# Down products with the low part last, and a row maximum queued behind a low part, in a fused feed-forward and attention kernel

## The chip, the cores and the metric

The kernel runs on one core of a Trainium2 chip. The metric is device time in microseconds (us), the median of several executions. A core has five engines that work side by side, each through its own queue in order: TensorE (PE in the profile; its weight loads are PEld), VectorE (DVE), ScalarE (ACT), GpSimd (POOL) and SyncE (SP, which here issues DMAs). An instruction waits at the head of its queue for what it needs, and everything behind it waits with it.

## The reference

A feed-forward layer, an attention layer and the same feed-forward layer again, each added to its input, on 4096 tokens of 256 features:

```python
x = x + 0.5 * ffn(layernorm(x))
x = x + attn(layernorm(x))
x = x + 0.5 * ffn(layernorm(x))

def ffn(x):
    # routed: 8 experts, each token to its 2 best, at most 640 tokens an expert
    gate = silu(einsum('ech,ehi->eci', xg, rg))
    up = einsum('ech,ehi->eci', xg, ru)
    eout = einsum('eci,eih->ech', gate * up, rd)
    # shared, for every token, 2048 inner features
    shared = silu(x @ sg) * (x @ su) @ sd
    return shared + routed

def attn(x):
    # groups of 64 tokens, 16 heads of 16 features, causal; q and k are normalised
    att = softmax(where(causal, q @ k.T / 4, -big))
    return (att @ v) @ w_proj
```

Inputs and result are float32.

## The kernel before

**Two-part numbers.** Every operand of a large product is kept as two 16-bit floats, a high part and what the high part leaves, the low part. A product of two such operands is made of three matmuls, in the order of `TERMS` (L35): high by high, high by low, low by high, the first of a pair being the left operand.

**Four phases.** Phase a (to about 268 us): the shared feed-forward part of blocks 0 to 3 of the first layer (a block is 512 tokens), with the normalising and routing of all tokens beside it. Phase b (to 590): the 8 experts of the first layer. Phase c (to 1420): the shared part of the first layer's blocks 4 to 7 and of the second layer's blocks 0 to 6, with the 32 attention tiles (128 tokens each) and the second layer's routing beside it. Phase d: the experts of the second layer and its last shared block.

**A chunk.** The inner features go by chunks of 128: 16 in a shared block, 8 in an expert. `gate_up` (L350) makes six matmuls of the gate into one PSUM bank, six of the up part into the next (`pgu`, a ring of three banks, L50). Of the gate comes `sl`: with `tanh` set, as in phase c, a Tanh on ACT (L367) and an addition and product on DVE (L368); else a Silu on ACT (L371). DVE multiplies by the up part (L373), ACT casts the product to its high part `hh` (L375), and DVE subtracts to make the low part `hl` (L376). `shared` and `experts` put off the chunk's down products by one chunk: `defer` (L97) keeps them and emits those of the chunk before.

**The down products.** `down` (L379) goes through the token tiles of a chunk (4 in a shared block, 5 in an expert) and makes three matmuls for each, with `hh`, `hh` and `hl` on the left, all of them adding to the tile's half of a PSUM bank. A block has two such banks, an expert three. They are read after the last chunk: L417 in a shared block (two instructions on DVE), L507 and L509 in an expert (on ACT and DVE).

**An attention tile.** `attn_tile` (L567) is a generator, written as a row of steps: load and normalise, q, k and v products, q and k to a layout with doubled rows (`QK`, L616 to L624), transposes by DMA, scores and mask (L636, L639), the maximum of each row of scores (`amx`, L644, on DVE over 128 x 1024 values), its subtraction (L645, POOL), the exponential (L653, ACT), the split of it into two parts (L655, L656), a transpose by DMA (`ET`), the products with v (`py`, L667), the normalising (L670, L673), the output product (`pao`), the second layer's normalising and routing products (`pl`). Its steps run in turns with those of a shared block: `drive` (L783) takes one round of tile steps for every three steps of the block, which is one chunk.

**What sets the order.** The program's text is only the order in which instructions are handed over. A scheduler that models each engine's time puts every engine's queue together; it may place any instruction ahead of another that it doesn't depend on, on PE too, so that in the built queue the matmuls of one `down` stand between those of other groups. Two means bind it: what an instruction reads and writes, and `issue_after`, which places an instruction behind a given one in its engine's queue (used by `behind`, L200).

Of the kernel before, what the change touches and what calls it, by code (L numbers as in the profile page):

```python
# [14 lines left out]
AF = mybir.ActivationFunctionType  # L15
ALU = mybir.AluOpType
AX = mybir.AxisListType
# [3 lines left out]
P = 128  # L21
H = 256
# [4 lines left out]
XP = UP * WS  # L27
# [10 lines left out]
class Net:  # L38
    def __init__(self, ctx, tc):
        self.tc = tc  # L40
        self.nc = nc = tc.nc
        pool = lambda name, bufs, **k: ctx.enter_context(tc.tile_pool(name=name, bufs=bufs, **k))
        self.cst = pool("cst", 1)
        self.wsh = pool("wsh", 1)
        self.tok = pool("tok", YB)
        self.xb = pool("xb", NB)
        self.xe = pool("xe", 2)
        self.sm = pool("sm", 2)
        self.dr = pool("dr", 1, space=DRAM)
        self.ps_gu = pool("ps_gu", 3, space=PSUM)  # L50
        self.pend = None
        self.latest = None
        self.anchor = None
        c = self.cst
        self.tri = c.tile([P, P], BF16, name="tri")
        nc.gpsimd.memset(self.tri, 1.0)
        nc.gpsimd.affine_select(
            out=self.tri, in_=self.tri, pattern=[[1, P]], compare_op=ALU.is_gt,
            fill=0.0, base=0, channel_multiplier=-1)
        self.ones = c.tile([P, P], BF16, name="ones")  # L60
        nc.gpsimd.memset(self.ones, 1.0)
        self.iota8 = c.tile([P, E], F32, name="iota8")
        for e in range(E):
            nc.gpsimd.memset(self.iota8[:, e:e + 1], float(e))
        self.mhalf = c.tile([P, 8], F32, name="mhalf")
        nc.gpsimd.memset(self.mhalf, -0.5)
        self.mone = c.tile([P, 4], F32, name="mone")
        nc.gpsimd.memset(self.mone, -1.0)
        self.e1 = c.tile([P, 4], F32, name="e1")
        nc.gpsimd.memset(self.e1, 2.718281828459045)  # L70
        warm = c.tile([P, 8], F32, name="warm")
        nc.scalar.activation(warm, self.mhalf, AF.Silu)
        tk = self.sm.tile([P, 32], I32, name="tk", bufs=1)
        nc.gpsimd.iota(tk, pattern=[[P, 32]], base=0, channel_multiplier=1)
        self.tokid = c.tile([P, 32], F32, name="tokid")
        nc.vector.tensor_copy(self.tokid, tk)
# [273 lines left out]
    def gate_up(self, wc, x, h, tanh=False):  # L350

        nc = self.nc
        n = x.shape[-1]
        ps = []
        for i in range(2):
            p = self.ps_gu.tile([P, n], F32, name="pgu", tag="gu")
            j = 0
            for k in range(2):
                for (w, a) in TERMS:
                    nc.tensor.matmul(  # L360
                        p, lhsT=wc[:, w, i, k, :], rhs=x[:, 2 * a + k, :], start=(j == 0), stop=(j == 5))
                    j += 1
            ps.append(p)
            if i == 0:
                s = self.hp.tile([P, BT], F32, name="sl", bufs=self.nsl)[:, :n]
                if tanh:
                    nc.scalar.activation(s, p, AF.Tanh, scale=0.5 / XP)  # L367
                    nc.vector.scalar_tensor_tensor(  # L368
                        out=s, in0=s, scalar=1.0, in1=p, op0=ALU.add, op1=ALU.mult)
                else:  # L370
                    self.latest[0] = nc.scalar.activation(s, p, AF.Silu, scale=1.0 / XP).ins  # L371
                yield
        self.latest[1] = nc.vector.scalar_tensor_tensor(  # L373
            out=s, in0=ps[1], scalar=1.0 / XP / (2.0 * XP if tanh else 1.0), in1=s, op0=ALU.mult, op1=ALU.mult).ins
        nc.scalar.copy(h[0], s)  # L375
        nc.vector.tensor_tensor(out=h[1], in0=s, in1=h[0], op=ALU.subtract)  # L376
        yield

    def down(self, outs, nt, h, wd, c, nch):  # L379
        nc = self.nc  # L380
        for t in range(nt):
            o = outs[t // 2][:, (t % 2) * H:(t % 2 + 1) * H]
            for j, (a, w) in enumerate(TERMS):
                nc.tensor.matmul(  # L384
                    o, lhsT=h[a][:, t * P:(t + 1) * P], rhs=wd[:, w],
                    start=(c == 0 and j == 0 and t % 2 == 0), stop=(c == nch - 1 and j == 2),
                    skip_group_check=True)

    def hbuf(self):
        hh = self.hp.tile([P, self.ntok], F16, name="hh")  # L390
# [176 lines left out]
    def attn_tile(self, R, j, x2, new_fb):  # L567

        nc = self.nc
        a = self.at  # L570
# [21 lines left out]
        for i in range(2):  # L592
            nc.scalar.activation(qk[:, i, :], pqk[:, i, :], AF.Square, scale=1.0 / XP, accum_out=ss[:, i:i + 1])
        nc.vector.tensor_scalar(
            out=ss, in0=ss, scalar1=XP ** 2 / H, scalar2=1e-6 * XP ** 2, op0=ALU.mult, op1=ALU.add)
# [6 lines left out]
            out=vs[:, 1, :], in0=pv, scalar=1.0 / XP, in1=vs[:, 0, :], op0=ALU.mult, op1=ALU.subtract)  # L602
        yield
        yield
        for i in range(2):
            nc.vector.scalar_tensor_tensor(
                out=qk[:, i, :], in0=pqk[:, i, :], scalar=ss[:, i:i + 1], in1=self.lnw,
                op0=ALU.mult, op1=ALU.mult)
        QS = self.QK[:, 0:16].rearrange("p (j s) (r a c) -> p j s r a c", s=2, r=2, a=4)
        for i in range(2):  # L610
            if i == 0:
                for r in range(2):
                    src = qk[:, 0, :].rearrange("p (j r c) -> p j r c", r=2, c=16)[:, :, r, :]
                    src = src.unsqueeze(2).to_broadcast([P, 8, 2, 16])
                    s = QS[:, :, r, r]
                    nc.scalar.copy(s[:, :, 0:2, :], src)  # L616
                    self.anchor = nc.gpsimd.tensor_tensor(
                        out=s[:, :, 2:4, :], in0=src, in1=s[:, :, 0:2, :], op=ALU.subtract)
            else:
                s = self.QK[:, 16:24].rearrange("p j (r a c) -> p (j r) a c", r=2, a=4)  # L620
# [3 lines left out]
                    out=s[:, :, 1::2, :], in0=src, in1=s[:, :, 0::2, :], op=ALU.subtract)  # L624
        yield
        QT = a.tile([P, 2, 24, 64], F16, name="QT")
        for g in range(2):
            nc.sync.dma_start_transpose(
                out=QT[:, g], in_=self.QK[g * 64:(g + 1) * 64].rearrange("p j c -> p (j c)"))
        yield  # L630
        yield
        S = a.tile([P, 16, 64], F32, name="S")
        for g in range(2):
            p = self.m1([P, 8, 64], F32, "psc")
            for jj in range(8):
                nc.tensor.matmul(  # L636
                    p[:, jj, :], lhsT=QT[:, g, 2 * jj:2 * jj + 2, :].rearrange("p r q -> p (r q)"),
                    rhs=QT[:, g, 16 + jj, :], start=True, stop=True)
            nc.vector.tensor_tensor(  # L639
                out=S[:, g * 8:(g + 1) * 8, :], in0=p,  # L640
                in1=self.mask.unsqueeze(1).to_broadcast([P, 8, 64]), op=ALU.add)
        yield
        mx = self.sm.tile([P, 16], F32, name="amx")
        nc.vector.tensor_reduce(out=mx, in_=S, axis=AX.X, op=ALU.max)  # L644
        self.anchor = nc.gpsimd.tensor_tensor(  # L645
            out=S, in0=S, in1=mx.unsqueeze(2).to_broadcast([P, 16, 64]), op=ALU.subtract)
        for g in range(2):
# [15 lines left out]
        for g in range(2):  # L663
# [7 lines left out]
            for r in range(2):  # L671
                sl = slice(r * 64, (r + 1) * 64)
                nc.vector.tensor_tensor(  # L673
                    out=Y[sl, g], in0=py[sl, :, r * 16:(r + 1) * 16],
                    in1=rc[sl].unsqueeze(2).to_broadcast([64, 8, 16]), op=ALU.mult)
# [253 lines left out]
```

## Time and profile before

| | |
|---|---|
| median of three runs | 1802.04 us (1801.54 to 1802.3) |
| the profiled execution | 1801.58 us |
| its span, first to last instruction | 1799.6 us |
| mean granted clock of TensorE | 0.999 |

The profile is of that one execution. "Busy" is the time in which an engine had an instruction under way; a matmul's end is modelled, since matmuls are pipelined. A line of a group, wait or timeline names the source line, the engine, the operation, and the tiles as out<-in; what stands behind "<-" in brackets is what the engine waited for and how long. The costliest groups show what a chunk costs on the other engines: L376 on DVE 618 ns in the mean over 512, L373 588 over 512, L375 on ACT 534 over 512, L368 682 over 176, and the maximum L644 1212 over 32. The down products are 4992 matmuls of 273 ns modelled length (2048, 1024, 1280 and 640 by operands), each with a weight load of 98 ns.

### The profile page before, as it was taken

Reading aid. Unit: us, or ns where it says so; the run is one execution under the profiler, and the core shown is the slowest. Engines: PE = TensorE matmul, PEld = TensorE weight load, DVE = VectorE, ACT = ScalarE, POOL = GpSimd, SP = SyncE. Lnnn points to the kernel's source line nnn. Section 1 sums busy time; section 2 is a strip of 40 time slices with the busy share of each in tenths; the row PEclk is TensorE's granted clock in tenths of the full one; section 3 lists DMA queues with packets and bytes.
Section 4 is the critical chain, followed back from the end, with each engine's and each line's share of the span. In section 5 each row is a group of like instructions: output and inputs, shape, how many; then the busy total and the mean of one; then the engine's idle time right before and its main releaser. Section 6 shows DMA issues by size and latency. Waiting matters only on the chain.

```text
span 1799.6 us, 37358 instructions
## 1 busy us (share of the span) xinstructions
PE 1773.4 (99%) x13652; PEld 1199.9 (67%) x13652; DVE 1194.3 (66%) x2905; ACT 951.3 (53%) x2053; POOL 753.5 (42%) x1072
## 2 busy tenths in 40 slices
PE   9999999999999999999999999999999999999998
PEld 5666667777777556665666666566656677777765
DVE  7766546666665668877787778777755566666643
ACT  5433335555554456666666666666333455555542
POOL 3677711211112345676767677676430011122210
PEclk9999999999999999999999999999999999999999
DMA  7334134555543356767676675856212154455420
GB/s 226 105 100 116 39 52 112 119 120 118 115 109 68 70 100 102 131 122 137 124 133 139 115 151 109 147 100 125 60 21 55 39 115 110 110 125 119 103 43 13
DMA packets 437545, 185.16 MB, mean 103 GB/s; under 512 B 302193, under 2 KB 434733, under 8 KB 437360
## 3 DMA queue, kind: packets, MB, share of 16 engines
q1 hardware_dynamic: 418880, 160.81, 40.9%
q0 software_dynamic: 17664, 21.17, 7.0%
q8 instruction: 107, 1.75, 0.4%
q10 hardware_dynamic: 816, 0.79, 0.1%
q14 instruction: 78, 0.64, 0.1%
HBM read 78.16 MB, written 42.21 MB: 67 GB/s over the span
## 4 chain that ended last, share of the span: by engine, by line
PE 40%; POOL 9%; DVE 8%; ACT 5%; issue 5%; DMA 2%; SPq 0%; POOLq 0%; DVEq 0%; ACTq 0%
PE pgu L360 25%; PE po L384 13%; POOL xg L341 2%; DVE hl L376 1%; DVE sl L368 1%; POOL S L645 1%; DVE amx L644 1%; ACT V L649 1%; DMA y<-acc 1%; DVE S L639 1%; ACT sl L367 1%; POOL e L656 1%; DVE sl L373 1%; POOL X L339 1%; POOL rstd L150 1%
## 5 line engine op out<-in xcount | busy, mean ns | idle before, releaser
L360 PE MATMUL pgu<-xb,sgu 128*128 128x512 f16 x3072 | 734.4, 379 | 6.4 <-DVE sl L368 5.6
L375 ACT CAST hh<-sl 128x512 f16<-128x512 f32 (+2 forms) x512 | 273.0, 534 | 544.8 <-DVE sl L373 540.0
L360 PE MATMUL pgu<-xe,wc 128*128 128x384 f16 (+1 forms) x3072 | 497.0, 299 | 0.0
L373 DVE SCALAR_TENSOR_TENSOR sl<-pgu,sl 128x512 f32<-128x512 f32 (+2 forms) x512 | 301.1, 588 | 269.4 <-PE pgu L360 236.2
L360 PEld LDWEIGHTS <-sgu 128*128 128x128 f16 x3072 | 292.7, 98 | 277.0 <-issue 9.0
L376 DVE TENSOR_TENSOR hl<-sl,hh 128x512 f16<-128x512 f32 (+2 forms) x512 | 316.4, 618 | 153.0 <-ACT hh L375 151.6
L384 PEld LDWEIGHTS <-hh 128*128 128x128 f16 x3328 | 321.5, 98 | 104.7 <-ACT hh L375 1.4
L360 PEld LDWEIGHTS <-wc 128*128 128x128 f16 x3072 | 300.6, 98 | 91.9
L384 PE MATMUL po<-sdw,hh 128*128 128x256 f16 x2048 | 349.7, 272 | 1.0 <-ACT hh L375 0.6
L384 PE MATMUL po<-sdw,hl 128*128 128x256 f16 x1024 | 249.1, 273 | 9.9 <-DVE hl L376 9.6
L384 PE MATMUL po<-wd,hh 128*128 128x256 f16 x1280 | 221.7, 273 | 0.0
L510 POOL DMA_INDIRECT out_dram<-eo,eidscatter x40 | 64.6, 1616 | 339.6 <-DVE eo L509 305.7
L371 ACT ACTIVATE sl<-pgu 128x384 f32<-128x384 f32 (+1 forms) x336 | 159.1, 474 | 76.5 <-PE pgu L360 49.7
L384 PEld LDWEIGHTS <-hl 128*128 128x128 f16 x1664 | 162.7, 98 | 51.1 <-DVE hl L376 16.4
L510 POOL DMA_INDIRECT acc<-eo,eidscatter x40 | 64.9, 1622 | 290.6 <-DVE eo L509 257.2
L368 DVE SCALAR_TENSOR_TENSOR sl<-sl,pgu 128x512 f32<-128x512 f32 x176 | 120.1, 682 | 57.0 <-ACT sl L367 55.9
L341 POOL DMA_INDIRECT xg<-X,di x128 | 133.5, 1043 | 45.6 <-issue 22.7
L384 PE MATMUL po<-wd,hl 128*128 128x256 f16 x640 | 147.9, 273 | 0.0
L367 ACT ACTIVATE sl<-pgu 128x512 f32<-128x512 f32 x176 | 104.4, 593 | 31.9 <-PE pgu L360 30.4
L105 ACT ACTIVATE wc<-re 128x512 f16<-128x512 f32 x124 | 78.1, 630 | 60.6 <-PE pgu L360 59.9
L106 DVE SCALAR_TENSOR_TENSOR wc<-re,wc 128x512 f16<-128x512 f32 x124 | 85.6, 690 | 13.9 <-ACT wc L105 13.9
L645 POOL TENSOR_TENSOR S<-S,amx 128x1024 f32<-128x1024 f32 x32 | 63.7, 1991 | 70.3 <-DVE amx L644 69.9
(159 smaller groups left out, 1729.1 us busy)
## 6 DMA issues: line engine op xcount, KB each, us to landing
re<-in_L_ffn_rg_dram SPq DMA_DIRECT2D x124, 128.0 KB, 2.3
re<-in_L_ffn_ru_dram SPq DMA_DIRECT2D x124, 128.0 KB, 2.5
re<-in_L_ffn_rd_dram SPq DMA_DIRECT2D x124, 128.0 KB, 2.5
y<-acc SPq DMA_DIRECT2D x64, 128.0 KB, 2.4
y<-in_L_attn_x_dram SPq DMA_DIRECT2D x32, 128.0 KB, 2.1
acc<-xr SPq DMA_DIRECT2D x16, 256.0 KB, 2.3
out_dram<-xr SPq DMA_DIRECT2D x16, 256.0 KB, 3.1
x<-y SPq DMA_DIRECT2D x28, 128.0 KB, 2.0
```

The lines of the kernel that those rows point to most:

```text
L106: nc.vector.scalar_tensor_tensor(out=lo, in0=src, scalar=WS, in1=hi, op0=ALU.mult, op1=ALU.subtract)
L341: i = nc.gpsimd.indirect_dma_start(out=R["xg"][:, :], out_offset=bass.IndirectOffsetOnAxis(ap=di[:, t, k:k + 1], axis=0), in_=X, in_offset ...
L360: nc.tensor.matmul(p, lhsT=wc[:, w, i, k, :], rhs=x[:, 2 * a + k, :], start=(j == 0), stop=(j == 5))
L367: nc.scalar.activation(s, p, AF.Tanh, scale=0.5 / XP)
L368: nc.vector.scalar_tensor_tensor(out=s, in0=s, scalar=1.0, in1=p, op0=ALU.add, op1=ALU.mult)
L371: self.latest[0] = nc.scalar.activation(s, p, AF.Silu, scale=1.0 / XP).ins
L373: self.latest[1] = nc.vector.scalar_tensor_tensor(out=s, in0=ps[1], scalar=1.0 / XP / (2.0 * XP if tanh else 1.0), in1=s, op0=ALU.mult, op ...
L375: nc.scalar.copy(h[0], s)
L376: nc.vector.tensor_tensor(out=h[1], in0=s, in1=h[0], op=ALU.subtract)
L384: nc.tensor.matmul(o, lhsT=h[a][:, t * P:(t + 1) * P], rhs=wd[:, w], start=(c == 0 and j == 0 and t % 2 == 0), stop=(c == nch - 1 and j == 2),
L510: i = nc.gpsimd.indirect_dma_start(out=R["acc"][:, :], out_offset=bass.IndirectOffsetOnAxis(ap=ids[:, t:t + 1], axis=0), in_=eo, in_offset ...
L645: self.anchor = nc.gpsimd.tensor_tensor(out=S, in0=S, in1=mx.unsqueeze(2).to_broadcast([P, 16, 64]), op=ALU.subtract)
```

## The change

`down` takes the three terms as its outer loop and the token tiles as the inner one: first high by high for every tile, then high by low, then low by high. In the first chunk of a block or an expert (`c == 0`) it does so for two tiles at a time, that is for one PSUM bank. The list `lows` collects the instructions that make low parts, and the maximum over a tile's scores is placed behind the last but one of them in DVE's queue. The list `looks` is filled but not read.

```diff
+        self.lows, self.looks = [], []
...
-                    nc.scalar.activation(s, p, AF.Tanh, scale=0.5 / XP)
+                    self.looks.append(nc.scalar.activation(s, p, AF.Tanh, scale=0.5 / XP).ins)
...
-        nc.vector.tensor_tensor(out=h[1], in0=s, in1=h[0], op=ALU.subtract)
+        self.lows.append(nc.vector.tensor_tensor(out=h[1], in0=s, in1=h[0], op=ALU.subtract).ins)
...
     def down(self, outs, nt, h, wd, c, nch):
-        nc = self.nc
-        for t in range(nt):
-            o = outs[t // 2][:, (t % 2) * H:(t % 2 + 1) * H]
+        nc = self.nc
+        step = 2 if c == 0 else nt
+        for t0 in range(0, nt, step):
             for j, (a, w) in enumerate(TERMS):
-                nc.tensor.matmul(
-                    o, lhsT=h[a][:, t * P:(t + 1) * P], rhs=wd[:, w],
-                    start=(c == 0 and j == 0 and t % 2 == 0), stop=(c == nch - 1 and j == 2),
-                    skip_group_check=True)
+                for t in range(t0, min(t0 + step, nt)):
+                    nc.tensor.matmul(
+                        outs[t // 2][:, (t % 2) * H:(t % 2 + 1) * H], lhsT=h[a][:, t * P:(t + 1) * P], rhs=wd[:, w],
+                        start=(c == 0 and j == 0 and t % 2 == 0), stop=(c == nch - 1 and j == 2),
+                        skip_group_check=True)
...
         mx = self.sm.tile([P, 16], F32, name="amx")
-        nc.vector.tensor_reduce(out=mx, in_=S, axis=AX.X, op=ALU.max)
+        with self.tc.issue_after(self.lows[-2]):
+            nc.vector.tensor_reduce(out=mx, in_=S, axis=AX.X, op=ALU.max)
```

## The prediction, made before the changed kernel ran

> **What bounds the kernel now.** I read the page's first part, then the stages, then the timeline of the one stage that is not full. The page says that PE is the bound, and which waits break it:
>
> ```profile
> PE 1773.4 (99%) x13652; PEld 1199.9 (67%) x13652; DVE 1194.3 (66%) x2905; ACT 951.3 (53%) x2053; POOL 753.5 (42%) x1072
> ...
> L384 PE MATMUL po<-sdw,hl 128*128 128x256 f16 x1024 | 249.1, 273 | 9.9 <-DVE hl L376 9.6
> ```
>
> The windows by stage (columns: start and end, length, busy time of PE, PEld, DVE, ACT, POOL, then clock and DMA) put the holes into one stage:
>
> ```profile
> 18.00:268.00 250.00, 250.00 (x1679) 152.72 (x1677) 156.08 (x489) 101.59 (x210) 147.11 (x308) 1.00 0.36 92
> 268.00:590.00 322.00, 321.61 (x2538) 248.09 (x2536) 202.94 (x451) 174.32 (x408) 63.34 (x39) 1.00 0.48 107
> 590.00:1420.00 830.00, 812.73 (x6462) 508.27 (x6461) 604.93 (x1452) 478.65 (x990) 469.93 (x648) 1.00 0.55 105
> 1420.00:1732.00 312.00, 312.00 (x2486) 242.94 (x2484) 194.20 (x431) 168.33 (x394) 56.94 (x35) 1.00 0.47 106
> ```
>
> The shared blocks of phase a and both runs of experts lose nothing; phase c, where the attention tiles run beside the shared blocks, loses 17.3 us. A matmul's modelled end hides part of a hole, so I went through PE's timeline of phase c by starts: 256 columns take 109 ns to the next start, 512 take 216 (the medians over 4991 and 3072 of them), and what is longer is a hole. From 818 us on, phase c repeats itself every 81.5 us (one shared block of 16 chunks beside four attention tiles), with four holes each time. **Hole A**, once a block, in the timeline at 838:
>
> ```profile
> 836.88 0.68 DVE L639 TENSOR_TENSOR S<-psc,mask 128x512 f32<-128x512 f32 x1
> 837.00 0.62 ACT L375 CAST hh<-sl 128x512 f16<-128x512 f32 x1 [1.95 <-DVE sl L373]
> 837.60 1.22 DVE L644 TENSOR_REDUCE amx<-S 128x16 f32<-128x1024 f32 x1
> 838.36 0.38 PE L384 MATMUL po<-sdw,hh 128*128 128x256 f16 x2
> 838.73 0.68 DVE L376 TENSOR_TENSOR hl<-sl,hh 128x512 f16<-128x512 f32 x1
> 838.90 2.28 POOL L645 TENSOR_TENSOR S<-S,amx 128x1024 f32<-128x1024 f32 x1 [2.47 <-DVE amx L644]
> 839.47 0.28 PE L384 MATMUL po<-sdw,hl 128*128 128x256 f16 x1 [0.73 <-DVE hl L376]
> ```
>
> hh was ready at 837.62, but VectorE did the maximum (1.22) first, so the low part came late: two hh products from 838.36 should end at 838.58, and the first hl product starts at 839.47, 0.89 later. **Hole B**, at 878:
>
> ```profile
> 877.72 0.97 POOL L341 DMA_INDIRECT xg<-X,di  x1 [0.30 <-issue]
> 878.17 1.10 DVE L376 TENSOR_TENSOR hl<-sl,hh 128x512 f16<-128x512 f32 x1
> 878.55 0.38 PE L384 MATMUL po<-sdw,hh 128*128 128x256 f16 x2
> 879.34 0.28 PE L384 MATMUL po<-sdw,hl 128*128 128x256 f16 x1 [0.40 <-DVE hl L376]
> ```
>
> Here the maximum already stands behind hl; hl itself is long. **Holes C and D**, at the change of block:
>
> ```profile
> 895.38 1.46 PE L360 MATMUL pgu<-xb,sgu 128*128 128x512 f16 x6
> 895.73 0.71 ACT L616 CAST QK<-qk 128x256 f16<-128x256 f32 x2 [0.65 <-DVE qk L606]
> 896.34 0.59 ACT L367 ACTIVATE sl<-pgu 128x512 f32<-128x512 f32 x1
> 896.97 0.69 DVE L368 SCALAR_TENSOR_TENSOR sl<-sl,pgu 128x512 f32<-128x512 f32 x1 [0.55 <-ACT sl L367]
> 897.71 1.46 PE L360 MATMUL pgu<-xb,sgu 128*128 128x512 f16 x6 [0.87 <-DVE sl L368]
> 899.56 0.68 DVE L417 SCALAR_TENSOR_TENSOR xr<-po,xr 128x512 f32<-128x512 f32 x1
> 900.16 0.68 DVE L376 TENSOR_TENSOR hl<-sl,hh 128x512 f16<-128x512 f32 x1
> 900.90 0.28 PE L384 MATMUL po<-sdw,hl 128*128 128x256 f16 x1 [0.71 <-DVE hl L376]
> ```
>
> C: the up products of chunk 1 need the bank of chunk 0's gate, whose Tanh waited on ACT behind attention casts: 895.38 + 6 x 0.216 = 896.68 against 897.71, 1.03. D: chunk 0's hl stands behind L417 twice and L639; two hh products from 899.81, and 0.87 lost.
>
> **The change, part by part.** It adds no instruction and no byte: all engine queues of the two builds hold the same instructions. They stand in another order, which the scheduler made, so I laid the built queues side by side.
>
> (1) *Low products last.* In chunks 1 to 15 all 8 hh products now stand ahead of the 4 hl ones, where in most chunks 2 to 4 did. At A and B 8 stand there instead of 2: 6 x 0.109 = 0.65 more cover. At D (chunk 0, two tiles at a time) 4 instead of 2: 0.22. Elsewhere in phase c I added, chunk by chunk, the shift of the first hh and first hl product (in PE work since the chunk's up products) to the distance that the trace shows between the ready operand and its use. In the repeating blocks none outside the holes falls below 0.7; two chunks near 650 us come out under zero, by less than 0.1, as new waits. The number of weight loads stays (one of 98 ns for each of 4992 down products, under 109 ns).
>
> (2) *The maximum behind hl.* In VectorE's queue this moves the maximum past an hl in 7 of 32 tiles, the sites A; in the others it already stands behind the hl that the change names. There hl comes 1.21 us earlier (the mean of L644), behind it nothing shifts, since the same two instructions end at the same time. The maximum comes 0.68 later; who waits for it is POOL's L645, then ACT's exponential, the casts, the transposes of ET and, on PE, the py products. Cover: in the tightest tile of the trace those start 1.9 us after ET landed; without it the 7 tiles would cost up to 7 x 0.68 = 4.8.
>
> Terms, against the profiled execution (1801.58; span 1799.6 and 1.98 around it):
> - A, seven sites (at 757, 838, 920, 1002, 1083, 1165, 1246: 0.35, 0.89, 0.90, 0.90, 0.90, 0.89, 0.19) = 5.0. 1.21 and 0.65 exceed each: all gone, -5.0 (bounds -5.0 and 0).
> - First 130 us of phase c: at 641 0.58 (hh) and 0.55, at 672 0.66, at 686 0.27, at 713 0.36 = 2.4. First products move back 0.62 and 1.27 (at 641), then hl by 0.76, 0.65, 0.38: -2.4 (0 if the new order of the first two attention tiles, whose qk products move up by 8 to 9 us, opens a hole as large).
> - B, six sites (0.19, 0.57, 0.16, 0.17, 0.16, 0.18) = 1.4, covered by 0.65: -1.4.
> - D: 6 x 0.22 = -1.3 of 5.2.
> - C: the edit doesn't touch it, but the order on ACT does: the squares of q and k (0.36 to 0.37 each, with accumulator reads) now stand ahead of both z (0.60), and the last cast (L622, 0.61) ahead of the Tanh. By hand at 891: squares from 891.6 to 892.4 and not 894.2; L594 at 893.1 behind nm; POOL's power 893.3 to 893.9; L606 to 894.9; casts to 895.8; Tanh at 895.8, not 896.34; L368 0.57 earlier. Bounds: 0.61 worse, if only the cast counts, to 1.03 better; I take -0.57 x 6 = -3.4, the value followed through rows.
> - Given back: POOL is busy without a pause that PE could shorten from 865.65 to 892.64 (the e of one tile, scatters, L645, the next e, rstd), and C waits for that rstd. What B saves PE inside this stretch makes PE wait longer at C: +1.4. A lies ahead of it, and at 864.15 POOL idles 3.66 us for the cast of yp, which hangs on PE's py products: A is kept.
> - Tail: PE ends 0.28 earlier, the first L417 starts 0.08 earlier: -0.1.
>
> Sum: -5.0 - 2.4 - 1.4 - 1.3 - 3.4 + 1.4 - 0.1 = -12.2, so 1789.4 for the profiled execution; the median of the runs lies 0.46 above that execution, so 1789.8: I say **1790**. Phase a and the experts have no hole to lose, and the distances counted there stay above 0.4 us: 0.
>
> The Trainium skill (SBUF — State Buffer, Who interferes with whom) says that a VectorE instruction with two SBUF inputs and a GpSimd instruction that reads SBUF shut each other out, the first holding the port to its end, and that a tensor_reduce never contends. The trace agrees: in hole B hl has 1.10 against 0.69 (median of hl rows with POOL idle), and the longest of all is 2.20. By that rule the swap puts the instruction that can be blocked where the one stood that can't.
>
> **The rivals.**
> *hl blocked in its new place*: if at A a POOL instruction stood beside the new hl, it could take 2.20, 1.5 longer; 1.21 + 0.65 - 1.5 leaves 0.36 of each 0.9 won, 2.5 for A instead of 5.0: 1792.3, and with a POOL instruction such as e (2.13) in every case 1794.8. Against: the row at 838.90 shows POOL idle for 2.47 us there.
> *POOL sets the pace*: if the attention chain and not PE decides, A and B are paid back at C, and C's reordering wins nothing: left are 2.4 + 1.3 + 0.1 = 3.8, so 1797.8. For it: the stretch of 27 us above. Against: the 3.66 us of POOL idle ahead of it.
> *It doesn't do what it says*: what PE waits for is not hl but something that comes as late, and the holes keep their size: 1802. Against: hl ends 0.06 ahead of the first hl product in each case.
> *Slower*: the 12 products of a chunk now stand as one block, and 62 groups of six gate or up products in phase c are cut by a whole block, 21 before. A cut gate's Tanh comes up to 1.31 later while the group that reuses its bank comes no later: in each block four groups have their distance from the group three earlier cut, from 5.5 to 7.8 us to 5.1 to 7.1. C's bank was released 5.19 us after its group. If release behind those cuts gets longer than 5.1 to 5.8, each waits like C: 4 x 6 x 1.03 = 24.7, less 12.2: 1814. Against: C's release is the slowest, and the other banks are not behind the attention casts.
>
> **How the numbers follow.** Forecast (1785 to 1794) 0.66; POOL's pace 0.12; hl blocked 0.05; no effect 0.06; slower 0.11. Less than 0.2%, 3.6 us, can't be told from no change. Forecast, hl blocked and two thirds of POOL's pace are faster: 0.79; the rest of it with no effect: 0.10 same; 0.11 slower. The range: below, C gone whole (2.8 more) and nothing given back (1.4): 1785. Above, C worse (3.4 + 3.7 less): 1797, POOL's pace 1798.2 on the runs' scale: 1799.
>
> **What would show it.** Right: PE's wait on hl (9.6) falls below 5, and what is left stands at the change of block; the maximum stands behind hl in every tile; the blocks of phase c come every 79.8 us instead of 81.5. C shows at the second group of a block: 0.5 to 1.0. Wrong: new waits of PE on L368 or L373 at cut groups, or C longer than 1.03 by what A and B gave.

## The result, and the profile after

The changed kernel takes 1792.85 us (median of 5 runs, 1792.66 to 1793.34); the kernel before, on the same chip, 1801.97 (1801.54 to 1802.3). The ratio is 0.9951, 95% interval 0.994 to 0.9962. The forecast was 1790, in a range of 1785 to 1799. The profiled execution took 1792.66, its span 1791.0, with a granted clock of 0.999 as before.

The first lines are from the page of the changed kernel: engines, then the down products of the low part (busy and mean ns of one; idle time of PE just before them, and what ended it).

```profile
PE 1772.8 (99%) x13652; PEld 1201.0 (67%) x13652; DVE 1190.0 (66%) x2905; ACT 944.3 (53%) x2053; POOL 747.1 (42%) x1072
...
L387 PE MATMUL po<-sdw,hl 128*128 128x256 f16 x1024 | 157.0, 273 | 3.9 <-DVE hl L377 3.8
```

Every engine has as many instructions as before, and the wait on the low part has gone from 9.6 to 3.8. That the group is busy for 157.0 instead of 249.1 is no saving: four hl products now stand side by side, and their modelled lengths overlap.

The windows by stage, with the borders moved by the 9 us that phase c became shorter:

```profile
18.00:268.00 250.00, 250.00 (x1676) 152.54 (x1675) 157.37 (x491) 100.71 (x211) 149.04 (x309) 1.00 0.36 93
268.00:590.00 322.00, 321.18 (x2536) 247.91 (x2534) 202.19 (x450) 170.83 (x409) 64.33 (x39) 1.00 0.47 107
590.00:1411.00 821.00, 811.75 (x6467) 508.99 (x6465) 601.46 (x1452) 480.03 (x990) 461.99 (x648) 1.00 0.57 106
1411.00:1723.00 312.00, 312.00 (x2483) 242.80 (x2482) 193.55 (x431) 164.88 (x394) 56.22 (x35) 1.00 0.47 106
```

PE is idle in phase c for 9.25 us (821.00 less 811.75), where it was 17.3. The other stages are as full as they were (321.18 of 322 for the experts, 321.61 before).

As in the prediction, I took each distance between the starts of two neighbouring matmuls, less what the first takes (109 ns for 256 columns, 216 for 512), and call what exceeds 0.1 us a hole. From 18 us to the end:

| holes, us | before | changed |
|---|---|---|
| start of phase c, 575 to 790 us | 6.12 | 7.84 |
| repeating blocks, 790 to 1260 us | 17.52 | 6.99 |
| elsewhere | 0.64 | 0.68 |
| sum | 24.28 | 15.51 |

The sum falls by 8.8 and the span by 8.6, so the holes account for the time. The blocks won more than forecast, the start of phase c got worse.

**Hole A is gone.** Timeline of the changed kernel at 838, the place shown of before:

```profile
837.67 0.68 DVE L377 TENSOR_TENSOR hl<-sl,hh 128x512 f16<-128x512 f32 x1
...
838.27 1.21 DVE L648 TENSOR_REDUCE amx<-S 128x16 f32<-128x1024 f32 x1
...
839.75 0.93 PE L387 MATMUL po<-sdw,hh 128*128 128x256 f16 x7
```

The maximum (L648) stands behind hl (L377). hl is done at 838.35, 1.4 us before even the first hh product; before, PE waited 0.73 for it with only two products ahead of it.

**Holes C and D**, at the change of block:

```profile
893.60 0.70 POOL L599 TENSOR_TENSOR ss<-ss,mhalf 128x2 f32<-128x2 f32 x1 [0.50 <-DVE ss L597]
...
894.33 0.88 DVE L609 SCALAR_TENSOR_TENSOR qk<-pqk,ss,lnw 128x256 f32<-128x256 f32 x2 [0.81 <-POOL ss L599]
...
895.35 0.39 PE L639 MATMUL psc<-QT 128*128 128x64 f16 x8 [0.42 <-DVE qk L609]
...
895.99 0.59 ACT L368 ACTIVATE sl<-pgu 128x512 f32<-128x512 f32 x1
...
896.61 0.69 DVE L369 SCALAR_TENSOR_TENSOR sl<-sl,pgu 128x512 f32<-128x512 f32 x1 [0.47 <-ACT sl L368]
```

C (the up products of chunk 1 behind L369) is 0.25 in each block, not 1.03. Ahead of it stands a new hole of 0.18 to 0.59: the second group of score products needs the PSUM bank that L609 reads, and that hangs on POOL's L599, as C did before. D, one block earlier:

```profile
819.27 0.68 DVE L420 SCALAR_TENSOR_TENSOR xr<-po,xr 128x512 f32<-128x512 f32 x1
...
819.51 0.60 PE L387 MATMUL po<-sdw,hh 128*128 128x256 f16 x4
819.86 0.68 DVE L377 TENSOR_TENSOR hl<-sl,hh 128x512 f16<-128x512 f32 x1
...
820.60 0.39 PE L387 MATMUL po<-sdw,hl 128*128 128x256 f16 x2 [0.49 <-DVE hl L377]
```

hl still stands behind the second read of the old block (L420). Four hh products stand ahead of it instead of two, and the hole is 0.65 instead of 0.87.

**The start of phase c** has holes at two places where before had smaller ones. The first:

```profile
633.16 0.40 ACT L172 CAST xa<-z 128x256 f16<-128x256 f32 x1 [3.68 <-DMA xt<-xa]
633.47 2.50 ACT L653 COPY V<-vs 64x512 f16<-64x512 f16 x4
...
635.99 0.71 ACT L619 CAST QK<-qk 128x256 f16<-128x256 f32 x2
...
636.61 0.61 ACT L625 CAST QK<-qk 128x512 f16<-128x512 f32 x1
637.13 0.61 ACT L376 CAST hh<-sl 128x512 f16<-128x512 f32 x1
...
637.72 1.16 POOL L626 TENSOR_TENSOR QK<-qk,QK 128x512 f16<-128x512 f32 x1
637.77 1.66 DVE L377 TENSOR_TENSOR hl<-sl,hh 128x512 f16<-128x512 f32 x1 [6.08 <-ACT hh L376]
...
637.79 1.05 PE L387 MATMUL po<-sdw,hh 128*128 128x256 f16 x8 [1.62 <-ACT hh L376]
...
639.49 0.61 PE L387 MATMUL po<-sdw,hl 128*128 128x256 f16 x4 [0.64 <-DVE hl L377]
```

Read it from the end: PE waits for hh, then for hl. hh stands on ACT behind the copies of V and the casts of q and k, and all of these behind a cast into `xa`, which has one buffer and waits until the DMA transpose of the tile before has read it. ACT did nothing for 3.68 us, and PE lost 1.78 ahead of hh. The 0.81 behind it is hl's own: hl takes 1.66 beside POOL's L626, where the median of hl with POOL idle is 0.69. At 0.69 it would have ended at 638.46, ahead of the eighth hh product's end (637.79 + 8 x 0.109 = 638.66), and by these rows no hole would be there. L626 is POOL's part of the cast of k; it falls beside hl because the casts of q and k stand just ahead of hh. The second place:

```profile
672.95 2.13 POOL L660 TENSOR_TENSOR e<-S,e 128x1024 f16<-128x1024 f32 x1 [4.63 <-ACT e L659]
...
673.73 1.89 DVE L377 TENSOR_TENSOR hl<-sl,hh 128x512 f16<-128x512 f32 x1 [2.10 <-ACT hh L376]
...
675.55 0.63 DVE L597 TENSOR_SCALAR ss<-ss 128x2 f32<-128x2 f32 x1
676.09 0.41 DVE L604 SCALAR_TENSOR_TENSOR vs<-pv,vs 128x256 f16<-128x256 f32 x1
...
676.55 0.39 PE L639 MATMUL psc<-QT 128*128 128x64 f16 x8 [1.53 <-DVE vs L604]
```

hl takes 1.89 beside POOL's e, and L604, which frees a bank for score products, is queued behind it. PE loses 1.69. Before lost 1.20 at this place in two parts (0.66 for hl, 0.54 for L604). The score products stand ahead of the hl products in PE's queue, so moving the low part back took the first wait away, and PE came to the second one earlier.

### The profile page after: what moved, and what is told of

Read it like the earlier page. It is cut to its first block, busy times and chain, and to the rows that moved or that the text cites. A ratio compares the mean times of both kernels' runs of the same rounds, so it can differ in the third digit from the quotient of the medians.

```text
span 1791.0 us, 37351 instructions
## 1 busy us (share of the span) xinstructions
PE 1772.8 (99%) x13652; PEld 1201.0 (67%) x13652; DVE 1190.0 (66%) x2905; ACT 944.3 (53%) x2053; POOL 747.1 (42%) x1072
## 4 chain that ended last, share of the span: by engine, by line
PE 88%; DVE 3%; POOL 3%; ACT 2%; issue 2%; DMA 1%; SPq 0%; DVEq 0%; POOLq 0%; ACTq 0%
PE pgu L361 55%; PE po L387 28%; PE pqk L702 2%; PE pao L702 1%; PE py L671 1%; PE pv L702 1%; DVE hl L377 1%; DVE sl L369 1%; DMA QT<-QK 1%; PE psc L639 1%; DVE xr L420 1%; DVE sl L374 0%; POOL xg L342 0%; ACT hh L376 0%; ACT sl L368 0%
## 5 line engine op out<-in xcount | busy, mean ns | idle before, releaser
L361 PE MATMUL pgu<-xb,sgu 128*128 128x512 f16 x3072 | 719.6, 379 | 2.2 <-DVE sl L369 1.2
L377 DVE TENSOR_TENSOR hl<-sl,hh 128x512 f16<-128x512 f32 (+2 forms) x512 | 313.9, 613 | 154.2 <-ACT hh L376 151.1
L387 PE MATMUL po<-sdw,hh 128*128 128x256 f16 x2048 | 270.4, 272 | 1.8 <-ACT hh L376 1.8
L387 PE MATMUL po<-wd,hh 128*128 128x256 f16 x1280 | 190.3, 273 | 0.0
L369 DVE SCALAR_TENSOR_TENSOR sl<-sl,pgu 128x512 f32<-128x512 f32 x176 | 120.0, 682 | 67.2 <-ACT sl L368 66.9
L387 PE MATMUL po<-sdw,hl 128*128 128x256 f16 x1024 | 157.0, 273 | 3.9 <-DVE hl L377 3.8
L387 PE MATMUL po<-wd,hl 128*128 128x256 f16 x640 | 115.2, 273 | 0.0
```

Of the source, the lines that this page charges most:

```text
L361: nc.tensor.matmul(p, lhsT=wc[:, w, i, k, :], rhs=x[:, 2 * a + k, :], start=(j == 0), stop=(j == 5))
L369: nc.vector.scalar_tensor_tensor(out=s, in0=s, scalar=1.0, in1=p, op0=ALU.add, op1=ALU.mult)
L377: self.lows.append(nc.vector.tensor_tensor(out=h[1], in0=s, in1=h[0], op=ALU.subtract).ins)
L387: nc.tensor.matmul(outs[t // 2][:, (t % 2) * H:(t % 2 + 1) * H], lhsT=h[a][:, t * P:(t + 1) * P], rhs=wd[:, w], start=(c == 0 and j == 0 a ...
```

## The experiments

Each kernel is compared with runs of the kernel before on its own chip, which took 1801.49 us for experiments 1 and 2, 1804.90 for 3 and 4, and 1801.29 for 5. All edits are against the changed kernel, if not said otherwise. Holes are counted as in the table above.

**1. The parts alone.** Down products with the low part last, without the bound maximum:

```diff
-        with self.tc.issue_after(self.lows[-2]):
-            nc.vector.tensor_reduce(out=mx, in_=S, axis=AX.X, op=ALU.max)
+        nc.vector.tensor_reduce(out=mx, in_=S, axis=AX.X, op=ALU.max)
```

> The low products last, the maximum not bound. In the built queue of VectorE the maximum stands behind the low part at the sites A all the same: with the low products later the scheduler puts it there by itself. On ACT the Tanh of hole C stands ahead of the three casts of QK, the squares of q and k behind z, X and xa. Theory of the holes (PE is the bound, the time is its work and its holes): A and B gone, D 0.65, C 0.25 or less, start of phase c unknown: 1790 to 1793. Theory that the bound maximum brings its own 5 us: 1797 to 1798.

Measured 1798.79 us, ratio 0.9985 (0.9976 to 0.9994). That is outside both ranges and nearer to the rival's; the trace says otherwise. From 901 us to 1225 us it has the holes of the changed kernel, place by place, to within 0.11: with low last, the scheduler by itself puts the maximum behind hl there. Of the 6.0 us of holes that it has more, 4.9 lie at the start of phase c (12.72 against 7.84) and the rest at the first change of block (814 and 824) and at 1246. The first tiles stand in an order that neither kernel has, and there a cast into `xa` that waits for its DMA stands ahead of a Tanh that PE needs. Its timeline on ACT:

```profile
660.98 0.40 ACT L172 CAST xa<-z 128x256 f16<-128x256 f32 x1 [3.77 <-DMA xt<-xa]
661.29 0.59 ACT L368 ACTIVATE sl<-pgu 128x512 f32<-128x512 f32 x1
```

PE lost 1.95 there. Other holes of that start have other causes: 1.62 at 652 stands behind a Tanh that follows a table load (1.28) and an exponential (1.06) on ACT, 1.84 at 682 behind L604, which is queued behind an hl of 1.89. What the bound maximum is worth stayed open until experiment 5.

The bound maximum alone, with the old order of down products:

```diff
     def down(self, outs, nt, h, wd, c, nch):
...
-        step = 2 if c == 0 else nt
-        for t0 in range(0, nt, step):
+        for t in range(nt):
+            o = outs[t // 2][:, (t % 2) * H:(t % 2 + 1) * H]
             for j, (a, w) in enumerate(TERMS):
-                for t in range(t0, min(t0 + step, nt)):
...
```

> The maximum bound behind the low part, the down products in the old order. Holes: A gone (7 sites, 5.0), D 0.87, C 1.03 (ACT's order there is that of before), B as before: 1797, between 1795.5 and 1798. Theory that the attention chain through POOL sets the pace: 1801 to 1802, since nothing of that chain comes earlier and the maximum comes 0.68 later in 7 tiles.

Measured 1796.96, ratio 0.9972 (0.9961 to 0.9984), as expected. Its timeline at the place of hole A:

```profile
838.09 0.69 DVE L377 TENSOR_TENSOR hl<-sl,hh 128x512 f16<-128x512 f32 x1
...
838.70 1.21 DVE L646 TENSOR_REDUCE amx<-S 128x16 f32<-128x1024 f32 x1
...
838.82 0.38 PE L385 MATMUL po<-sdw,hh 128*128 128x256 f16 x2
...
839.04 0.27 PE L385 MATMUL po<-sdw,hl 128*128 128x256 f16 x1
```

The hl product starts 0.22 after two hh products: no hole. All seven sites of A are closed, B stays (0.14 to 0.58), C (1.03) and D (0.87) are as before. The blocks lose 12.77 instead of 17.52. Nothing of A was paid back at C, where the rival by which POOL sets the pace said 1801 to 1802: for hole A that rival is refuted.

**2. Hole D.** Low last over the whole first chunk:

```diff
-        step = 2 if c == 0 else nt
+        step = nt
```

> The changed kernel, with the first chunk of a block term by term over all four tiles too, not two at a time. At D eight high products stand ahead of the first low one, not four. Holes: the high products of tiles 2 and 3 wait some 0.2 for their bank, which the second L417 frees at about the time when the low part begins, then cover the low part; hole D falls from 0.65 to 0.2 to 0.4, 6 sites: 1.5 to 2.7 less than the changed kernel, 1790.1 to 1791.3. Rival, that the bank and not the low part ends hole D: no gain, 1792.8 or more.

Measured 1790.61, ratio 0.9939 (0.9925 to 0.9952): as expected. D goes from 0.65 to 0.27, because the next products are then those of the second bank, which wait for L420: it ends at 820.16, and the first of these products starts at 820.21.

The second read behind the first low part:

```diff
+                    with self.tc.issue_after(self.lows[-1]) if i else nullcontext():
-                    nc.vector.scalar_tensor_tensor(
+                        nc.vector.scalar_tensor_tensor(
...
```

> The changed kernel, with the second L417 of a block bound behind the low part of the next block's first chunk: at D VectorE's queue reads L417, L639, hl, L417. Simple theory (hole D is the low part's lateness alone): hl 0.6 earlier, 6 sites, 3.6 less than the changed kernel: 1789.2. Theory of two holes: the second bank comes free 0.6 later, and the high products of tile 2, behind the low ones of tiles 0 and 1, wait 0.4 for it: 0.43 left of 0.65, 1.3 less: 1791.5.

Measured 1791.31, ratio 0.9945 (0.9931 to 0.9958), as the theory of two holes has it. Its timeline, with the read now in L421:

```profile
819.14 0.68 DVE L377 TENSOR_TENSOR hl<-sl,hh 128x512 f16<-128x512 f32 x1
...
819.39 0.60 PE L387 MATMUL po<-sdw,hh 128*128 128x256 f16 x4
819.74 0.68 DVE L421 SCALAR_TENSOR_TENSOR xr<-po,xr 128x512 f32<-128x512 f32 x1
...
820.48 0.60 PE L387 MATMUL po<-sdw,hh 128*128 128x256 f16 x4 [0.20 <-DVE xr L421]
```

The wait on hl is gone, and the wait on the bank took its place, 0.37 of 0.65. DVE has two results to deliver there, and PE waits for whichever comes second.

**3. The start of phase c.** A second buffer for `xa`:

```diff
-        xa = a.tile([P, 2 * H], F16, name="xa")
+        xa = a.tile([P, 2 * H], F16, name="xa", bufs=2)
```

> The changed kernel with a second buffer for xa (the attention input that is transposed by a DMA), so that ACT's cast xa of tile 1 need not wait until the transpose of tile 0 has landed. Nothing else is edited; near 634 us that cast now stands right behind the one before, and hh and the 12 products behind it stand in the same order. Theory 'a cast that waits for a DMA stands ahead of hh on ACT': the hole of 1.78 ahead of the hh products at 636 falls under 0.4 and the hl wait of 0.81 behind it under 0.4; 2.0 to 2.6 less, 1790.3 to 1790.9. Rival 'the first attention tiles set the pace': the hole moves on to the next group that needs them, the holes from 583 to 760 us still sum to 7.2 or more, and the time is 1792.2 to 1793.4.

Measured 1793.39, where the kernel before took 1804.90 (1804.08 to 1806.61): ratio 0.9937 (0.9923 to 0.995), which is 1790.6 where before takes 1801.97. The interval alone does not part it from the changed kernel's 0.9951. The holes do: 7.84 fall to 4.40 at the start. Timeline at the same place:

```profile
635.75 0.41 ACT L172 CAST xa<-z 128x256 f16<-128x256 f32 x1 [2.24 <-DMA xt<-xa]
...
636.07 0.61 ACT L376 CAST hh<-sl 128x512 f16<-128x512 f32 x1
...
636.71 0.74 DVE L377 TENSOR_TENSOR hl<-sl,hh 128x512 f16<-128x512 f32 x1 [4.35 <-ACT hh L376]
636.73 1.05 PE L387 MATMUL po<-sdw,hh 128*128 128x256 f16 x8 [0.45 <-ACT hh L376]
...
637.62 0.60 PE L387 MATMUL po<-sdw,hl 128*128 128x256 f16 x4
```

With two buffers it is a later tile's cast that waits, for 2.24, and hh stands right behind it. The hole ahead of hh is 0.62 (under 0.4 was expected), that ahead of hl is gone, as hl takes 0.74 and not 1.66, and one of 0.50 follows at L369.

The same buffer in the kernel before:

> The kernel before with the same second buffer for xa. Its first tiles have no cast that waits for a DMA ahead of an hh that PE needs, so by the first theory the buffer is worth nothing by itself: 1801.0 to 1802.4. If the buffer helped in any order (a wait that both kernels have), it would take 2 us here too: 1799.5 or less.

Measured 1803.31, ratio 0.999 (0.9981 to 0.9999), by the medians 1.6 less. So the expectation was wrong: the start's holes fall from 6.12 to 4.01. The timeline of before at 640, read again, shows why:

```profile
640.58 0.40 ACT L171 CAST xa<-z 128x256 f16<-128x256 f32 x1 [4.00 <-DMA xt<-xa]
640.89 0.61 ACT L375 CAST hh<-sl 128x512 f16<-128x512 f32 x1
...
641.53 0.74 DVE L376 TENSOR_TENSOR hl<-sl,hh 128x512 f16<-128x512 f32 x1 [2.66 <-ACT hh L375]
...
641.56 0.39 PE L384 MATMUL po<-sdw,hh 128*128 128x256 f16 x2 [0.42 <-ACT hh L375]
```

The holes of 2.59 after the change (1.78 and 0.81) were 1.13 before (0.58 and 0.55), behind the same wait of `xa`. The change didn't make that wait; the new order put seven ACT instructions (4 copies of V, 3 casts of q and k) between the waiting cast and hh, and POOL's part of the last cast beside hl.

**4. Two more tries at the start, on the same chip.** Low last over the whole first chunk, with the first casts of q in tiles 0 to 3 bound behind the newest hh cast:

```diff
-        nc.scalar.copy(h[0], s)
+        self.highs.append(nc.scalar.copy(h[0], s).ins)
...
-                    nc.scalar.copy(s[:, :, 0:2, :], src)
+                    with self.tc.issue_after(self.highs[-1]) if j < 4 else nullcontext():
+                        nc.scalar.copy(s[:, :, 0:2, :], src)
```

> The version with the low part last in the first chunk too (1790.61, the base of comparison) with the first casts of q in tiles 0 to 3 bound behind the newest hh cast on ACT, xa left with one buffer. Near 634 us hh then stands behind the waiting xa cast and one cast of k, but ahead of the copies of V (2.49) and the casts of q (0.71): about 3 us earlier. Theory 'casts ahead of hh on ACT': the two holes of 1.79 and 0.81 go, 1788.0 (1787.5 to 1788.8). Rival 'the first attention tiles set the pace': the casts come later, so the transposes and the psc products do, and PE waits there instead: 1790.2 to 1792.

Measured 1793.12, ratio 0.9937 (0.9923 to 0.995). By the ratio nothing was won over its base (0.9939), as the rival has it. By the holes the start went from 8.42 to 5.22, as the first theory has it: the 1.79 ahead of hh became 0.58 and the 0.81 ahead of hl 0.14. Between the two readings stand 3.85 us of holes at 1271 to 1334, which all four profiles taken on this chip have in some size (2.68 to 3.85), the one of before with a second `xa` too, and no other profile of this study. By its time this run is inconclusive.

The first shared block of phase c with its down products in the old order:

```diff
-        step = 2 if c == 0 else nt
+        step = 1 if old else 2 if c == 0 else nt
...
-                self.down(outs, 4, h, self.sdw[:, :, c], c, 16)
+                self.down(outs, 4, h, self.sdw[:, :, c], c, 16, tanh and b == NA and src is dst)
```

> The changed kernel, with the down products of the first shared block of phase c (the only one beside the first four attention tiles) in the old order, tile by tile. If the order of the products is what makes the start worse (by the holes 583 to 760 us: 5.8 us before, 7.8 after), the start goes back to about 5 to 6 us and the time to 1790.0 to 1791.3. If the scheduler's order there is chance, and the bound maximum alone is enough to stir it, the start holds 7 to 10 us in some third order: 1792 to 1795.

Measured 1795.28, ratio 0.9947 (0.9933 to 0.996), with 5.45 of holes at the start. The holes agree with the first theory. The ratio, 1792.4 where before takes 1801.97, doesn't, and the 3.69 us at the end of phase c on this chip blur it. It is one more sample of an order and no proof.

**5. Together.** The changed kernel again, and three that use the second `xa`.

> The changed kernel once more, so that the others of this call have it on the same chip: 0.994 to 0.9962 of the kernel before, as in its first runs. No theory is tried by it.

Measured 1792.10 (1791.94 to 1793.47), ratio 0.995 (0.9936 to 0.9963), with 7.87 of holes at the start: the order there is fixed in the built kernel, and its cost repeats to 0.03 us.

Second `xa` and low last over the whole first chunk:

```diff
-        step = 2 if c == 0 else nt
+        step = nt
...
-        xa = a.tile([P, 2 * H], F16, name="xa")
+        xa = a.tile([P, 2 * H], F16, name="xa", bufs=2)
```

> The low part last over the whole first chunk too, and a second buffer for xa. Two theories of two separate waits: 0.35 to 0.4 less in each of six blocks (2.2 as run alone) and 3.4 less holes at the start of phase c (as run alone). If both add up, 5.6 less than the changed kernel (4.5 to 6.2), about 1787.2 where that takes 1792.8. If the second xa only moves the start's waits on (rival: its ratio of 0.9937 was within the interval of the changed kernel's), 2.2 less.

Measured 1787.58 (1786.43 to 1788.57), ratio 0.9921 (0.9907 to 0.9934). That is 4.5 us less than the changed kernel on the same chip, and the two intervals don't touch. The two parts add up, at the low end of what was expected: 2.5 at the start (holes 5.37; alone it was 3.4) and 2.0 in the blocks (5.02). The page has nothing left of the wait that the change was about:

```profile
L387 PE MATMUL po<-sdw,hl 128*128 128x256 f16 x1024 | 155.4, 273 | 0.1
```

Low last and second `xa`, maximum not bound: the diffs of experiments 1 and 3 together.

> Low part last without the bound maximum (1798.79 alone, where the changed kernel had 1792.85), with the second buffer for xa. In the repeating blocks its order is that of the changed kernel; all of the 6 us lay at the start of phase c. Theory 'the bound maximum is worth nothing by itself, and the loss came from casts behind the xa cast that waits for its buffer': the start's holes fall from 12 to about 4 to 5 us, and the time to that of the changed kernel with a second xa: 3 less to 1 more than the changed kernel. Rival 'the bound maximum does protect hl at the start': 3 us or more above the changed kernel.

Measured 1789.10 (1788.53 to 1789.44), ratio 0.9931 (0.9917 to 0.9944), 3.0 less than the changed kernel and 9.7 less than the same kernel with one `xa` (0.9985 there). The start's holes fall from 12.72 to 3.15. So what low last alone lost does not come from the missing bound on the maximum. Not all of it was the wait for that buffer: of the 9.6 us of holes that went, 4.55 stood behind casts into `xa` or in their wake (1.79, 0.81 and 1.95), and the 1.62 and 1.84 named in experiment 1, which have other causes, went with the order too. With two buffers the bound maximum is worth nothing that the times can tell: 0.9931 without it, 0.9937 with it (experiment 3, on the chip that loses time near the end of phase c). By the holes it is worth 0.6 in the blocks (7.9 without, 7.3 with) and nothing at the start (3.15 without, 4.40 with). In five tiles the maximum stands ahead of an hl here, with one hole of 0.38 and one of 0.18 to show for it.

The version with the first chunk and second `xa`, and QK in two copies as well:

```diff
-        self.QK = a.tile([P, 24, P], F16, name="QK")
-        nc.gpsimd.memset(self.QK, 0.0)
+        self.QKs = []
+        for i in range(2):
+            q = a.tile([P, 24, P], F16, name=f"QK{i}")
+            nc.gpsimd.memset(q, 0.0)
+            self.QKs.append(q)
...
+        QK = self.QKs[j % 2]
```

> As the version with the first chunk and the second xa, with QK (the layout that the second DMA transpose reads) in two copies too, so that neither cast of a tile waits for a transpose of the tile before. Theory 'after xa, the next wait at the start is QK's': 0.5 to 1.5 less again at the start (holes of 0.62 and 0.50 at 636 and 638, 0.80 at 673). Rival 'what is left there is the psc groups behind VectorE and the hh casts': within 0.5 of the version with xa alone, or above it where the new order opens others.

Measured 1787.72 (1787.44 to 1788.4), ratio 0.9925 (0.9911 to 0.9938): the rival, within 0.2 of the same version with one QK. The trace has something of both: the hole ahead of hh at 636 fell from 1.24 to 0.42, one of 1.04 ahead of hl opened at 600, and the start sums to 4.9 instead of 5.4. The hole of 0.79 that it keeps at 672 is the one behind hl and L604.

## Why the prediction came out as it did

The direction and the range were right, and the likeliest value was 2.9 us too low. Term by term, in holes, beside what was forecast:

| term | forecast | measured |
|---|---|---|
| A, seven sites | -5.0 | -5.0 |
| B, six sites | -1.4 | -1.4 |
| D, six sites | -1.3 | -1.3 (0.87 to 0.65) |
| C and what is given back | -3.4 + 1.4 = -2.0 | -3.1 (1.03 to 0.25 in six blocks, and 1.6 in new holes at L639) |
| first 130 us of phase c | -2.4 | +2.1 (5.77 to 7.84, from 575 to 790 us, without A's site at 757) |
| tail | -0.1 | -0.3 |
| first chunks of the experts | 0 | +0.3 (0.16 at 271 and at 1414) |
| sum | -12.2 | -8.7 |

Added up before rounding, the holes fall by 8.8.

**The term that was mis-sized is the first 130 us of phase c.** The working took the holes at 641, 672, 686 and 713, saw that the products move back in PE's queue by more than each, and wrote -2.4. It measured the distance from a ready operand to its use and left the ready time where it was. Its upper bound of 0 ("if the new order of the first two attention tiles ... opens a hole as large") was too near as well. The runs showed that at 641 the ready time was set on ACT, by a cast that waits for a DMA, and moving the products couldn't help against what the new order puts behind that cast: 1.78 ahead of hh, and 0.81 ahead of an hl that POOL lengthened. The idle time of ACT, 4.00 us ended by a DMA, was in the trace of before. For the repeating blocks I had followed ACT's order by hand, and there the forecast held but for the size of C; for the first tiles I had looked at PE's order alone. The hole at 672 was taken for one of hl alone; the wait for L604 behind the same hl was not in the sum.

**C was mis-sized the other way.** C itself fell by 0.78 a block and not by 0.57, and fell below the 0.5 to 1.0 named as its sign. What is given back showed, but ahead of C: the 0.18 to 0.59 at L639 hang on POOL's L599, whose place behind e and the two rstd the prediction had named. Each block comes 79.5 us after the one before (the up products behind C start at 897.35, 976.88, 1056.42: 79.5), where 79.8 was said.

**The signs named beforehand.** PE's wait on hl fell to 3.8, below 5, and 2.9 of it stands at the change of block (six times 0.49), right. No maximum is followed directly by an hl on DVE (seven were), right. No new wait of PE at cut gate or up groups in the blocks, so the rival that ended slower has no support in this trace; the bank releases behind such groups were not measured one by one.

**The other rivals.** POOL's pace fell with experiment 1, second kernel. "hl blocked in its new place" did not happen at A, where hl takes 0.68. At the start it did, in the rows of 1.66 and 1.89 above. The 1.66 is new (before, hl took 0.74 there), and it is PE's loss of 0.81. The 1.89 stood at the same place before. The trace agrees there with the Trainium skill (SBUF — State Buffer, Who interferes with whom), by which a VectorE instruction with two SBUF inputs and a GpSimd instruction that reads SBUF contend: hl, with two SBUF inputs, ends at 675.62, about half a microsecond after POOL's e at 675.08. What the 1.89 cost was decided by what stood behind hl in DVE's queue.

**The sum of the parts.** Alone, low last wins 2.7 us and the bound maximum 4.5 by the medians (1801.49 less 1796.96; 5.0 by its ratio); both win 9.1. With a second `xa`, low last alone (1789.10) wins more than both without it (1792.10 on that chip). An edit that changes an order can't be priced by its own sites only: each built order has its own luck at the start, with 3 to 13 us of holes in the kernels tried here.

## What to carry to other kernels

When an edit moves products later, check what makes their operand late and not only how much work now stands ahead of them: follow the operand to the head of its producer's queue, and see whether something there waits for a DMA or a buffer. Do this for each irregular stretch (the first tiles of a phase above all) and not only for the block that repeats, since a scheduler builds another order there from any small edit. A single-buffered tile between a cast and a DMA transpose is a cheap suspect: a second buffer was one word here, and took 3.4 of the 7.84 us of holes at the start.

## What the runs showed that was not expected

On the chip where the kernel before took 1804.90, all four profiles lose 2.7 to 3.9 us near the end of phase c, where the other ten lose nothing. In the changed kernel with the second `xa`:

```profile
1276.57 0.27 PE L387 MATMUL po<-sdw,hh 128*128 128x256 f16 x1
...
1277.89 0.94 PE L387 MATMUL po<-sdw,hh 128*128 128x256 f16 x7 [1.05 <-issue]
1278.09 0.60 ACT L368 ACTIVATE sl<-pgu 128x512 f32<-128x512 f32 x1 [1.31 <-PE pao L702]
```

PE stops between two products of one group, with operands that are ready, and waits for nothing that the profile shows ("issue"). Waits of this kind make 1.55 of the 3.7 us there; the other 2.1 stand behind instructions of DVE that came late (1.02 ahead of the `pao` products at 1276, 1.11 behind L369 at 1337). What it was is open; no run was made on it. It is the reason why, for experiments 3 and 4, holes by place tell more than the time.
